# Turning the next expert's rows ahead of the last output product in a mixture-of-experts stage

## The chip, the core and the metric

The kernel runs on one core of a Trainium2 chip. The time is the device time of an execution in microseconds (us), and the figure that counts is the median over several executions. TensorE (PE) multiplies matrices out of SBUF into PSUM; a weight load (PEld) goes ahead of each matmul. VectorE (DVE) and ScalarE (ACT) work elementwise and copy PSUM into SBUF, GpSimd (POOL) issues the indirect transfers here, and SyncE (SP) issues the plain ones.

## What is computed

One layer of a perceiver over 32 sequences of 32 tokens, 512 wide: cross-attention to a context, self-attention, and a feed-forward with 8 experts of which each token takes two. The change touches only the last part:

```python
gate_logits = jnp.einsum('td,ed->te', xf, gate_w)
gate_scores = jax.nn.sigmoid(gate_logits + balance_bias)
topk_scores, topk_idx = jax.lax.top_k(gate_scores, ACTIVE_EXPERTS)
topk_scores = topk_scores / (topk_scores.sum(axis=-1, keepdims=True) + 1e-06)
comb = jnp.zeros((T, NUM_EXPERTS), dtype=x.dtype)
comb = comb.at[jnp.arange(T)[:, None], topk_idx].add(topk_scores)
h = jax.nn.silu(jnp.einsum('td,ehd->teh', xf, w1))
expert_out = jnp.einsum('teh,edh->ted', h, w2)
out = jnp.einsum('te,ted->td', comb, expert_out)
```

There are 1024 tokens, `w1` is 8 x 1024 x 512 and `w2` 8 x 512 x 1024, all in float32. `xf` is the layer's input to this part after a normalization, and the result is added to the residual.

## The kernel before

The kernel computes only the chosen token-expert pairs. While self-attention runs, the normalized row of each token, with its number and its two shares, is scattered by GpSimd into a list per expert in DRAM (`xs_d`). A count near the end of that phase ranks the experts by size, and the place in this ranking, r, has a fixed width, `WIDTH = (384, 352, 288, 288, 288, 224, 192, 160)`; rows beyond these widths go to a branch that is taken only if there are any. The first 256 rows of the largest expert (`EARLY = 2` blocks of 128) are worked on inside the attention phase, between the last tiles of attention: `early_turn`, `early_hidden` eight times, and `early_out`. The names there are `xpe`, `phe` and `poe`.

Then come the experts in order of rank. For each:

- `load_rows` brings its rows into `xs` with the rows on partitions (two buffers).
- `turn_rows` (before: one function) turns each block of up to 128 rows with four TensorE transposes into PSUM (`xpt`), copies them to `xT` (even blocks on ScalarE, odd ones on VectorE, in `evac`, lines 175 to 179), and forms the row numbers `idx` and shares `share` on VectorE.
- `hidden` has eight groups of four matmuls `ph <- xT, w1` (line 1402), a sigmoid on ScalarE (`sg`), and a product on VectorE into `hT`. TensorE needs the whole of `xT` for the first group.
- `output` multiplies `hT` by `w2`. A whole block of 128 rows has eight matmuls of 512 columns (`fpo`, line 1464). A shorter last block is split over the array's columns (`fpq`, line 1369); it comes first, except for the last expert. VectorE scales by the share into `fob` (three buffers), and GpSimd adds the rows to the output with an indirect transfer (`add_rows`, line 195).

The remaining 128 rows of rank 0 (`rest`) have their own way: `hidden_of_block` makes the hidden values with the rows on partitions (`phb`, then `sgb` and `hs`, in two halves), and `turn_hidden` turns them (`hpt`) once the rows of rank 1 have been turned. Its output product stands after the hidden product of rank 1.

Each engine takes its instructions in the order in which the built program lists them. A scheduler forms that order out of the order of the calls; on TensorE it follows the calls in this stage. Buffers rotate: the pool `ps` has four PSUM tiles of one bank each, shared by `phe`, `xpt`, `phb`, `hpt`, `ph` and small ones, and `psf` four for the outputs of `output`. The early outputs before the change take one tile of four banks from `psq`, of which each uses one bank. The weights `w1` and `w2`, 2 MB each, rotate through three buffers; SP's queue issues, for rank r+1, `w1`, the rows and `w2` in this order, each when its buffer is free.

The trace counts two instructions for a float32 matmul call, and one for a transpose: a block's eight `fpo` matmuls show as 16 in it.

Of the kernel before, what the change touches and what calls it, by code (L numbers as in the profile page):

```python
# [9 lines left out]
F32 = mybir.dt.float32  # L10
# [7 lines left out]
P = 128  # L18
# [4 lines left out]
D = 512  # L23
DC = 384
KD = D // P
# [4 lines left out]
NE = 8  # L30
# [5 lines left out]
WIDTH = (384, 352, 288, 288, 288, 224, 192, 160)  # L36
# [16 lines left out]
def tile_perceiver_layer(  # L53
# [28 lines left out]
    ps = ctx.enter_context(tc.tile_pool(name="ps", bufs=4, space=PSUM))  # L82
# [92 lines left out]
    def evac(i, o, src):  # L175
        if i % 2 == 0:
            nc.scalar.copy(o, src)  # L177
        else:
            nc.vector.tensor_copy(o, src)
# [14 lines left out]
    def add_rows(dst, ob, place, n):  # L194
        return nc.gpsimd.indirect_dma_start(  # L195
            out=dst,
            out_offset=bass.IndirectOffsetOnAxis(ap=place, axis=0),
            in_=ob,
            in_offset=None,
            bounds_check=n * ROWS - 1,  # L200
            oob_is_err=True,
            compute_op=ALU.add,
        )

    def load_expert(dst, src, e):

        n = src.shape[1] // 2
        for k in range(2):
            nc.sync.dma_start(
                dst.rearrange("p (h r) -> p h r", h=2)[:, k, :].rearrange(  # L210
                    "p (k f) -> p k f", f=src.shape[2]
                ),
                src[bass.ds(e, 1), ts(k, n), :].rearrange("e (k p) f -> p (e k) f", p=P),
            )

    def expert_w1(e, ewp=ewp):
        w1 = ewp.tile([P, KD * FF], F32, tag="ew", name="w1")
        load_expert(w1, w1T, e)
        return w1.rearrange("p (k f) -> p k f", f=FF)

    def expert_w2(e, ewp=ewp):
        w2 = ewp.tile([P, KF * D], F32, tag="ew", name="w2")
        load_expert(w2, w2T, e)
        return w2.rearrange("p (k f) -> p k f", f=D)

    with ExitStack() as attn:
# [19 lines left out]
        with ExitStack() as xa:  # L246
# [534 lines left out]
            for g in range(NTT + 1):  # L781
                p = g // 2
# [50 lines left out]
        with ExitStack() as sa:  # L833
            wk = sa.enter_context(tc.tile_pool(name="swork", bufs=2))
            psq = sa.enter_context(tc.tile_pool(name="psq", bufs=1, space=PSUM))
# [373 lines left out]

            def early_out():  # L1210
                t = tail["early"]
                pe = psq.tile([P, 4, KD, P], F32, tag="pq", name="poe")
                for c in range(EARLY):
                    po = pe[:, c].rearrange("p k q -> p (k q)")
                    for f in range(KF):
                        nc.tensor.matmul(  # L1216
                            po, t["hT"][f // 4][:, f % 4, ts(c, P)], tail["w2"][0][:, f, :],
                            start=(f == 0), stop=(f == KF - 1),
                        )
                    ob = wk.tile([P, NH * T], F32, tag="aT", bufs=3, name="obe")  # L1220
                    nc.vector.tensor_scalar_mul(ob, po, t["share"][:, c : c + 1])
                    add_rows(out, ob, t["pl"][:, c : c + 1], 1)
# [40 lines left out]
            p = NP - 1  # L1263
# [30 lines left out]
            for f in range(3, KF):  # L1294
                early_hidden(f)
            early_out()


# [5 lines left out]
    hot, eids, w1s, w2s = tail["hot"], tail["e"], tail["w1"], tail["w2"]  # L1304
# [8 lines left out]
    taken = keep.tile(full, I32, name="taken")  # L1313
# [3 lines left out]
    idx = keep.tile(full, I32, name="idx")  # L1317
    nc.gpsimd.iota(
        idx, pattern=[[0, NE], [P, LIST // P]], base=NTT * P, channel_multiplier=1
    )  # L1320
    def parts_of(n):
        return [(c, min(P, n - c * P)) for c in range((n + P - 1) // P)]

    def tails_of(m):

        return [(0, 2 * Q)] * (m // (2 * Q)) + [(m // Q * Q - Q, Q)] * (m // Q % 2)

    def load_rows(e, r0, n):

        xs = fw.tile([P, NB, YW], F32, tag="xs", name="xs")  # L1330
        nb, m = n // P, n % P
        if nb:
            nc.sync.dma_start(
                xs[:, 0:nb, :],
                xs_d[bass.ds(e * LIST + r0, nb * P), :].rearrange("(c p) w -> p c w", p=P),
            )
        if m:
            nc.sync.dma_start(
                xs[0:m, nb, :], xs_d[bass.ds(e * LIST + (r0 + nb * P), m), :]
            )  # L1340
        return xs
# [34 lines left out]

    def turn_rows(r, xs, n, taken, idx):

        share = fw.tile([P, NB], F32, tag="share", name="share")
        xT = fw.tile([P, KD, CAP], F32, tag="xT", name="xT")  # L1380
        for c, m in parts_of(n):
            pt = ps.tile([P, KD, P], F32, tag="ps", name="xpt")
            for k in range(KD):
                nc.tensor.transpose(pt[:, k, 0:m], xs[0:m, c, ts(k, P)], ident[0:m, 0:m])  # L1384
            evac(c, xT[:, :, c * P : c * P + m], pt[:, :, 0:m])
            nc.vector.copy_predicated(
                idx[0:m, c : c + 1], taken[0:m, c : c + 1],
                xs[0:m, c, YI : YI + 1].bitcast(I32),
            )
            sh = fw.tile([P, NE], F32, tag="sh", name="sh")  # L1390
            nc.vector.tensor_mul(sh[0:m], xs[0:m, c, YC : YC + NE], hot[0:m, r, :])
            nc.vector.reduce_sum(share[0:m, c : c + 1], sh[0:m], axis=AX.X)
        return {"n": n, "xT": xT, "share": share, "idx": idx}

    def hidden(t, w1):

# [20 lines left out]
    def hidden_of_block(t, w1):  # L1417

        hs = fw.tile([P, FF], F32, tag="hs", bufs=1, name="hs")
        for h in range(2):  # L1420
            ph = ps.tile([P, D], F32, tag="ps", name="phb")
            for k in range(KD):
                nc.tensor.matmul(  # L1423
                    ph, t["xT"][:, k, 0:P], w1[:, k, ts(h, D)],
                    start=(k == 0), stop=(k == KD - 1),
                )
            sg = fw.tile([P, D], F32, tag="sgb", bufs=1, name="sgb")
            nc.scalar.activation(sg, ph, AF.Sigmoid)
            nc.vector.tensor_mul(hs[:, ts(h, D)], ph, sg)
        t["hs"] = hs  # L1430
# [6 lines left out]
                nc.tensor.transpose(pt[:, k, :], t["hs"][:, ts(h * KD + k, P)], ident)  # L1437
            evac(h, t["hT"][:, h * KD : (h + 1) * KD, 0:P], pt)

    def output(t, w2, short_first=True):  # L1440

        hT, share, idx = t["hT"], t["share"], t["idx"]
        parts = parts_of(t["n"])
        adds = []

        def short():
            for c, m in parts:
                if m < P:
                    for r0, q in tails_of(m):
                        adds.append(  # L1450
                            short_part(
                                hT[:, :, c * P + r0 : c * P + r0 + q],
                                w2, q, *t["spread"].pop(0),
                            )
                        )

        if short_first:
            short()
        for c, m in parts:
            if m < P:  # L1460
                continue
            po = psf.tile([P, D], F32, tag="psf", name="fpo")
            for f in range(KF):
                nc.tensor.matmul(  # L1464
                    po, hT[:, f, ts(c, P)], w2[:, f, :],
                    start=(f == 0), stop=(f == KF - 1),
                )
            ob = fw.tile([P, D], F32, tag="fob", bufs=3, name="fob")
            nc.vector.tensor_scalar_mul(ob, po, share[:, c : c + 1])  # L1469
            adds.append(add_rows(out, ob, idx[:, c : c + 1], 1))  # L1470
        if not short_first:
            short()

            for i, a in enumerate(adds):
                for b in adds[:i]:
                    tc.declare_no_dep(a.ins, b.ins, reason="rows of their own")


    rows_of = {
        0: load_rows(eids[0], EARLY * P, WIDTH[0] - EARLY * P),  # L1480
        1: load_rows(eids[1], 0, WIDTH[1]),
    }
    w2s[1] = expert_w2(eids[1])
    rest = turn_rows(
        0, rows_of.pop(0), WIDTH[0] - EARLY * P, taken[:, 0, EARLY:], idx[:, 0, EARLY:]
    )
    hidden_of_block(rest, w1s.pop(0))
    for r in range(1, NE):
        if r + 1 < NE and r > 1:
            w1s[r + 1] = expert_w1(eids[r + 1])  # L1490
            rows_of[r + 1] = load_rows(eids[r + 1], 0, WIDTH[r + 1])
            w2s[r + 1] = expert_w2(eids[r + 1])
        t = turn_rows(r, rows_of.pop(r), WIDTH[r], taken[:, r], idx[:, r])
        if r == 1:
            turn_hidden(rest)
        hidden(t, w1s.pop(r))
        if r == 1:
            output(rest, w2s.pop(0))
            w1s[2] = expert_w1(eids[2])
            rows_of[2] = load_rows(eids[2], 0, WIDTH[2])  # L1500
            w2s[2] = expert_w2(eids[2])
        output(t, w2s.pop(r), r + 1 < NE)


    over = keep.tile([P, NE + 1], F32, name="over")
# [131 lines left out]
```

## Time and profile before

| what | us |
|---|---|
| median of three runs | 552.19 |
| the runs | 551.84, 552.19, 555.09 |
| the profiled execution | 559.04 |
| its span, first to last instruction | 557.3 |
| TensorE busy in the span | 520.1 |
| VectorE, ScalarE, GpSimd busy | 241.9, 123.2, 106.1 |
| mean granted TensorE clock | 0.985 |

The stages in that execution, by the chain of waits: attention up to about 304 us; the early output products 304.3 to 319.2; the rest of rank 0 and the turning of rank 1, 319.2 to 329.7; then rank 1 to 375.6, rank 2 to 409.4, rank 3 to 443.2, rank 4 to 476.9, rank 5 to 504.0, rank 6 to 527.2, rank 7 to 547.3, and the last row additions to the end. The bounds from 375.6 to 527.2 are the starts of the next expert's `xpt`.

A line of the profile names the program's line (L1402), the engine, the operation, what it writes and reads, how often, and times. A wait is given with the instruction that released it. Matmul ends are modelled, so that consecutive matmuls overlap in the list; the spacing of starts is what a stream of them costs.

### The profile page before, as it was taken

What the parts mean: (1) busy time and instruction counts of PE and PEld (TensorE: products, weight loads), DVE (VectorE), ACT (ScalarE), POOL (GpSimd) and SP (SyncE); (2) the same over time, 40 slices, a digit from 0 to 9 for tenths busy, and PEclk for the clock granted to TensorE, in tenths of its full rate; (3) what the DMA queues carried; (4) which work ended last, traced back from release to release, by engine and by line L of the source; (5) the groups of instructions that cost most, each with busy time, mean ns of one, the idle gap of its engine ahead of it and who ended that gap; (6) DMA issues with size and microseconds to landing.
All of it is one profiled execution on the core that took longest, in us unless ns stands there. A gap on an engine that the chain in (4) does not pass through costs nothing.

```text
span 557.3 us, 11309 instructions
## 1 busy us (share of the span) xinstructions
PE 520.1 (93%) x4718; PEld 337.6 (61%) x4718; DVE 241.9 (43%) x706; ACT 123.2 (22%) x274; POOL 106.1 (19%) x185
## 2 busy tenths in 40 slices
PE   6999998999989999999789899999999999999992
PEld 3655554556675774866368356547567475768571
DVE  6564668655676665778244132203113121223120
ACT  3444434322321412213031021002011020102010
POOL 2323446120001023031202100122111202112102
PEclk9899999999999999999799999999999999999997
DMA  8999977999931002021494250847463455756512
GB/s 279 393 379 403 303 266 269 360 393 386 387 124 39 2 19 100 4 80 41 157 396 160 68 162 9 285 95 231 158 192 114 125 181 158 217 162 198 163 21 28
DMA packets 43648, 104.56 MB, mean 188 GB/s; under 512 B 4002, under 2 KB 7234, under 8 KB 42563
## 3 DMA queue, kind: packets, MB, share of 16 engines
q1 hardware_dynamic: 38994, 94.96, 47.4%
q0 software_dynamic: 4592, 8.78, 7.8%
q8 instruction: 39, 0.64, 0.5%
q14 instruction: 23, 0.18, 0.1%
HBM read 75.55 MB, written 28.18 MB: 186 GB/s over the span
## 4 chain that ended last, share of the span: by engine, by line
PE 68%; DVE 3%; issue 2%; ACT 1%; POOL 0%; POOLq 0%; ACTq 0%
PE ph L1402 18%; PE fpo L1464 15%; PE pp L388 8%; PE ppv L858 4%; PE ppo L934 4%; PE fpq L1369 4%; PE phe L1202 3%; PE poe L1216 3%; PE pos L915 2%; PE pqs L873 1%; PE phb L1423 1%; PE xpt L1384 1%; PE pg L980 1%; ACT xT L177 1%; PE po L671 1%
## 5 line engine op out<-in xcount | busy, mean ns | idle before, releaser
L1402 PE MATMUL ph<-xT,w 128*128 128x288 f32 (+4 forms) x448 | 100.2, 382 | 3.1 <-ACT xT L177 3.1
L1402 PEld LDWEIGHTS ph<-xT,w 128*128 128x128 f32 x448 | 79.0, 190 | 19.6 <-ACT xT L177 3.7
L1464 PE MATMUL fpo<-w,hT 128*128 128x512 f32 x192 | 84.3, 595 | 0.0
L1464 PEld LDWEIGHTS fpo<-w,hT 128*128 128x128 f32 x192 | 35.9, 190 | 43.7 <-issue 43.5
L1408 DVE TENSOR_TENSOR hT<-ph,sg 128x288 f32<-128x288 f32 (+4 forms) x56 | 23.7, 422 | 63.9 <-ACT sg L1407 63.9
L1469 DVE TENSOR_SCALAR fob<-fpo,share 128x512 f32<-128x512 f32 x12 | 9.0, 751 | 75.9 <-PE fpo L1464 75.9
L1407 ACT ACTIVATE sg<-ph 128x288 f32<-128x288 f32 (+4 forms) x56 | 21.5, 384 | 85.0 <-PE ph L1402 83.5
L195 POOL DMA_INDIRECT out_dram<-fob,idx x12 | 18.6, 1548 | 106.3 <-DVE fob L1469 93.5
L934 PE MATMUL ppo<-ao,oT 128*128 128x512 f32 x64 | 31.0, 638 | 2.3 <-DVE oT L922 2.3
L528 DVE BATCH_NORM_STATS2 st<-n 128x6 f32<-128x384 f32 x64 | 32.5, 545 | 0.0
L177 ACT COPY xT<-xpt 128x512 f32<-128x512 f32 (+2 forms) x12 | 6.0, 496 | 112.5 <-PE xpt L1384 112.4
L195 POOL DMA_INDIRECT out_dram<-fob,plc x9 | 13.9, 1546 | 88.9 <-DVE fob L1374 71.2
L483 PE MATMUL pq<-x1T,mq 128*128 128x256 f32 x96 | 24.7, 406 | 0.0
L671 PE MATMUL po<-wvo,uT 128*128 128x512 f32 x48 | 22.4, 602 | 1.2 <-ACT uT L664 1.2
L934 PEld LDWEIGHTS ppo<-ao,oT 128*128 128x128 f32 x64 | 12.9, 205 | 17.4 <-issue 14.5
L1072 POOL DMA_INDIRECT xs_d<-fy,pi x16 | 17.2, 1073 | 30.1 <-DVE pi L1068 20.2
L388 PE MATMUL pp<-syT,ak 128*128 128x256 f32 x96 | 22.4, 385 | 0.3 <-issue 0.3
L1369 PE MATMUL fpq<-w,hT 128*32 128x128 f32 (+1 forms) x576 | 22.3, 309 | 0.0
L388 PE MATMUL pp<-syT,aq 128*128 128x256 f32 x96 | 22.1, 383 | 0.0
L858 PE MATMUL ppv<-av,syT 128*128 128x512 f32 x48 | 21.3, 594 | 0.0
L483 PEld LDWEIGHTS pq<-x1T,mq 128*128 128x128 f32 x96 | 18.5, 202 | 4.1 <-issue 1.2
L1369 PEld LDWEIGHTS fpq<-w,hT 128*32 128x32 f32 x576 | 16.2, 110 | 7.1 <-issue 3.2
(280 smaller groups left out, 734.7 us busy)
## 6 DMA issues: line engine op xcount, KB each, us to landing
xs_d<-zero SPq DMA_DIRECT2D x8, 2112.0 KB, 20.5
w<-in_w1T_dram SPq DMA_DIRECT2D x16, 1024.0 KB, 7.7
w<-in_w2T_dram SPq DMA_DIRECT2D x16, 1024.0 KB, 8.8
nT<-in_ctxT_dram SPq DMA_DIRECT2D x8, 1542.0 KB, 8.2
n<-in_ctx_dram SPq DMA_DIRECT2D x32, 384.0 KB, 5.9
xs<-xs_d SPq DMA_DIRECT2D x4, 528.0 KB, 9.4
x_sb<-in_x_dram SPq DMA_DIRECT2D x8, 256.0 KB, 7.5
out_dram<-x_sb SPq DMA_DIRECT2D x8, 256.0 KB, 2.1
```

Of the source, the lines that this page charges most:

```text
L195: return nc.gpsimd.indirect_dma_start(out=dst, out_offset=bass.IndirectOffsetOnAxis(ap=place, axis=0), in_=ob, in_offset=None, bounds_chec ...
L388: nc.tensor.matmul(pp[:, i, :], w[:, k, ts(e, P)], yT[:, k, :], start=(k == 0), stop=(k == KD - 1),)
L483: nc.tensor.matmul(pq[:, 0 : 2 * P], mq[:, k, ts(c, P)], x1T[:, k, :], start=(k == 0), stop=(k == KD - 1),)
L528: nc.vector.bn_stats(st[:, r, :], n[:, r // 2, r % 2, :])
L671: nc.tensor.matmul(po, uT[:, c, :], wvo[:, c, :], start=(c == 0), stop=(c == KC - 1))
L858: nc.tensor.matmul(pp, st[p]["yT"][:, k, ts(i, P)], av[:, k, :], start=(k == 0), stop=(k == KD - 1),)
L934: nc.tensor.matmul(pp, st[p]["oT", i][:, k].rearrange("p b q -> p (b q)"), ao[:, k, :], start=(k == 0), stop=(k == KD - 1),)
L1369: nc.tensor.matmul(po[ts(g, Q), 0:w], hT[:, f, ts(h, Q)], w2[:, f, ts(j, w)], start=(f == 0), stop=(f == KF - 1),)
L1402: nc.tensor.matmul(ph[:, 0:n], w1[:, k, ts(f, P)], t["xT"][:, k, 0:n], start=(k == 0), stop=(k == KD - 1),)
L1407: nc.scalar.activation(sg[:, 0:n], ph[:, 0:n], AF.Sigmoid)
L1408: nc.vector.tensor_mul(hT[:, f, 0:n], ph[:, 0:n], sg[:, 0:n])
L1464: nc.tensor.matmul(po, hT[:, f, ts(c, P)], w2[:, f, :], start=(f == 0), stop=(f == KF - 1),)
```

## The change

Three things are done. `turn_rows` is divided into `turning`, which takes the tiles, and `turn_parts`, which turns a choice of blocks. `output` takes a function `ahead`, called before the product of its last whole block; for rank r that function turns the rows of rank r+1. The rows of rank 1 have no output before them to go ahead of, and are turned in two pieces: the first block before `hidden_of_block(rest)` and the others after it. And `early_out` takes one tile of `ps` for each of its two products, in place of one tile of four banks for both.

In the built program, ranks 2 to 5 have their transposes between the first and the second `fpo` product of the expert before; ranks 6 and 7, whose predecessors have one whole block, have them between `fpq` and `fpo`. On VectorE the copy into `xT` comes one place earlier, ahead of the last `fob`; the `idx` and `share` operations of a later expert come one `hT` product later; and one copy into `xT` now stands between the two `hs` products. On ScalarE the first copy for rank 1 comes ahead of both `sgb`. The orders on SP and POOL are unchanged.

```diff
             def early_out():
                 t = tail["early"]
-                pe = psq.tile([P, 4, KD, P], F32, tag="pq", name="poe")
                 for c in range(EARLY):
-                    po = pe[:, c].rearrange("p k q -> p (k q)")
+                    po = ps.tile([P, D], F32, tag="ps", name="poe")
                     for f in range(KF):
                         nc.tensor.matmul(
                             po, t["hT"][f // 4][:, f % 4, ts(c, P)], tail["w2"][0][:, f, :],
...
     def turn_rows(r, xs, n, taken, idx):
 
+        t = turning(r, xs, n, taken, idx)
+        turn_parts(t)
+        return t
+
+    def turning(r, xs, n, taken, idx):
         share = fw.tile([P, NB], F32, tag="share", name="share")
         xT = fw.tile([P, KD, CAP], F32, tag="xT", name="xT")
-        for c, m in parts_of(n):
+        return {
+            "n": n, "r": r, "xs": xs, "xT": xT, "share": share, "idx": idx, "taken": taken,
+        }
+
+    def turn_parts(t, which=slice(None)):
+        xs, xT, share = t["xs"], t["xT"], t["share"]
+        r, idx, taken = t["r"], t["idx"], t["taken"]
+        for c, m in parts_of(t["n"])[which]:
             pt = ps.tile([P, KD, P], F32, tag="ps", name="xpt")
             for k in range(KD):
                 nc.tensor.transpose(pt[:, k, 0:m], xs[0:m, c, ts(k, P)], ident[0:m, 0:m])
...
-    def output(t, w2, short_first=True):
+    def output(t, w2, short_first=True, ahead=None):
...
-        for c, m in parts:
-            if m < P:
-                continue
+        blocks = [c for c, m in parts if m == P]
+        for c in blocks:
+            if ahead and c == blocks[-1]:
+                ahead()
             po = psf.tile([P, D], F32, tag="psf", name="fpo")
...
+    t = turning(1, rows_of.pop(1), WIDTH[1], taken[:, 1], idx[:, 1])
+    turn_parts(t, slice(0, 1))
     hidden_of_block(rest, w1s.pop(0))
+    turn_parts(t, slice(1, None))
     for r in range(1, NE):
-        if r + 1 < NE and r > 1:
-            w1s[r + 1] = expert_w1(eids[r + 1])
-            rows_of[r + 1] = load_rows(eids[r + 1], 0, WIDTH[r + 1])
-            w2s[r + 1] = expert_w2(eids[r + 1])
-        t = turn_rows(r, rows_of.pop(r), WIDTH[r], taken[:, r], idx[:, r])
+        n = r + 1
+        if n < NE and r > 1:
+            w1s[n] = expert_w1(eids[n])
+            rows_of[n] = load_rows(eids[n], 0, WIDTH[n])
+            w2s[n] = expert_w2(eids[n])
         if r == 1:
             turn_hidden(rest)
         hidden(t, w1s.pop(r))
         if r == 1:
             output(rest, w2s.pop(0))
-            w1s[2] = expert_w1(eids[2])
-            rows_of[2] = load_rows(eids[2], 0, WIDTH[2])
-            w2s[2] = expert_w2(eids[2])
-        output(t, w2s.pop(r), r + 1 < NE)
+            w1s[n] = expert_w1(eids[n])
+            rows_of[n] = load_rows(eids[n], 0, WIDTH[n])
+            w2s[n] = expert_w2(eids[n])
+        turned = []
+
+        def ahead():
+            if n < NE:
+                turned.append(
+                    turn_rows(n, rows_of.pop(n), WIDTH[n], taken[:, n], idx[:, n])
+                )
+
+        output(t, w2s.pop(r), n < NE, ahead)
+        t = turned[0] if turned else None
```

More of the change, by code (lines that the diff above doesn't have):

```diff
@@ L1392, in turn_rows @@
             nc.vector.reduce_sum(share[0:m, c : c + 1], sh[0:m], axis=AX.X)
-        return {"n": n, "xT": xT, "share": share, "idx": idx}
     def hidden(t, w1):
```

## The prediction, made before the changed kernel ran

> **What bounds the kernel now.** I read the page first: TensorE's row, the slices and the costliest groups. Then the waits of TensorE from 300 us to the end, the chain of waits for the same stretch, and last the timeline of two places.
>
> ```profile
> PE 520.1 (93%) x4718; PEld 337.6 (61%) x4718; DVE 241.9 (43%) x706; ACT 123.2 (22%) x274; POOL 106.1 (19%) x185
> ...
> PE   6999998999989999999789899999999999999992
> ...
> PEclk9899999999999999999799999999999999999997
> ...
> L1402 PE MATMUL ph<-xT,w 128*128 128x288 f32 (+4 forms) x448 | 100.2, 382 | 3.1 <-ACT xT L177 3.1
> ```
>
> TensorE is busy for 93% of the span. Each digit is a slice of 13.9 us; from 320 us on, where the experts are, it never falls below nine tenths until the last slice, and the 8 just before (306 to 320 us) is the end of the early expert. The clock is nine tenths or more there. So in the expert stage only TensorE's own work and its own holes count. The group row shows one kind of hole: 3.1 us before `ph`, ended by ScalarE's copy into `xT`. The waits of TensorE from 300 us on list all of them:
>
> ```profile
> PE ph L1402 <- ACT xT L177: 3.1, 6, 0.7
> PE poe L1216 <- DVE obe L1221: 0.8, 1, 0.8
> PE phb L1423 <- ACT xT L177: 0.7, 1, 0.7
> ```
>
> Columns: waiter, what it waited for, us in all, times, longest. That is 4.6 us in eight waits, the most that a reordering of this stage can give back by this list. In the chain (start us, us, engine, tile, line) they look so:
>
> ```profile
> 304.32 6.88 PE poe L1216 x16
> 311.22 0.76 DVE obe L1221
> 312.03 7.13 PE poe L1216 x16
> ...
> 319.64 0.59 ACT xT L177
> 320.27 7.13 PE phb L1423 x16
> ...
> 375.59 1.25 PE xpt L1384 x12
> 376.86 0.27 ACT xT L177
> 377.13 0.16 issue
> 377.30 4.12 PE ph L1402 x16
> ```
>
> TensorE turns an expert's rows (`xpt`, 1.25 us), has nothing else in its queue, and waits until the copies out of PSUM end. The chain has PE before and after each of these holes, so they lie on the path to the end.
>
> **The change part by part.** All sums are against the profiled execution: 559.04 us, span 557.3 and 1.7 around it. It lies 6.85 us above the median of the three runs shown (552.19). The holes are waits of one instruction for another, tens to hundreds of ns each, and I carry them over to the median unscaled.
>
> *Rows of experts 2 to 7 ahead of the last block's product.* No instruction is added: per expert the same 8 or 12 transposes, copies, `idx` and `share` operations. The built order shows what moves. On TensorE the transposes go ahead of the last 8 `fpo` products (16 matmuls in the trace). On VectorE the copy of the second 128 rows goes ahead of the last `fob`. On ScalarE nothing changes places, and the issues on SP's and POOL's queues are the same in the same order. The holes by expert, from the timeline: 0.47, 0.47, 0.47, 0.70, 0.56, 0.43, sum 3.10. Cover in their new place: one block's product, 7.0 us, against about 1.0 us for the last transpose's landing and its copy. So the holes go whole: -3.10. From the weight-load row the same six waits are 3.7 us, which is the upper end; the lower end is 2.7, if each expert's return from transposes to products costs 0.07 us more than a plain step. That is what the one switch shown costs (eight `hpt` start at 328.57 and `ph` at 329.50, 0.93 instead of 8 times 0.107).
>
> What could be late next? First, the rows themselves, since the transposes come 7 us sooner and the block's product is queued behind them. The `idx` operation on VectorE reads the same rows and shows when they land:
>
> ```profile
> 359.78 0.22 DVE L1386 COPY_PREDICATED_SCALAR idx<-taken,xs 128x1 int32 x1 [2.67 <-DMA xs<-xs_d]
> ```
>
> Expert 2's rows are there at 359.8, and their transposes would start at 368.7 on this clock: 8.9 us to spare. For expert 7 it is 513.3 at the latest against 520.1, 6.8 us; the others lie between or above. Second, VectorE's copy stands behind `fob` of the block before, which waits for the scatter three before it to free its buffer; in this trace every `fob` waited for TensorE (75.9 us of 75.9), and a delay costs only beyond the 5 us or so of cover. Third, the loads of the next weights start at an expert's end as before, but its successor's `ph` now starts 1.7 us sooner relative to that. The `idx` operations of the expert after stand one `hT` product later in VectorE's order, so they wait about as long as before (7.9 us in five waits), and TensorE did not wait for VectorE there. Cost of all three: 0.
>
> *A buffer for each early output.* Two tiles from the general pool of four take the place of the halves of one large tile. The second `poe` product no longer waits for the 0.76 us scaling of the first: -0.84 (312.03 less the end at 311.20). The new tiles take over from `phe` outputs whose readers ended before 302; the two after them in the ring are only written at about 319. No other wait comes in.
>
> *The second expert's rows around the first product of the rest.* Its first four transposes now stand ahead of `phb`. They do not bring `phb` forward: it waits for ScalarE's copy of its own rows, 1.27 us after the first transpose either way, and that copy is still first in ScalarE's queue. The hole of 0.68 us is just filled with 0.43 us of work, which then is missing after `phb`. There it was cover:
>
> ```profile
> 327.25 1.37 PE L1384 MATMUL xpt<-ident,xs 128*128 128x128 f32 x12
> 327.45 0.60 ACT L1428 ACTIVATE sgb<-phb 128x512 f32<-128x512 f32 x1 [2.84 <-PE phb L1423]
> 327.94 1.19 ACT L177 COPY xT<-xpt 128x512 f32<-128x512 f32 x2
> 328.08 0.69 DVE L1429 TENSOR_TENSOR hs<-phb,sgb 128x512 f32<-128x512 f32 x1 [2.74 <-ACT sgb L1428]
> 328.57 1.09 PE L1437 MATMUL hpt<-ident,hs 128*128 128x128 f32 x8
> 329.50 0.79 PE L1402 MATMUL ph<-xT,w 128*128 128x352 f32 x2
> ```
>
> Call E the end of `phb`, 327.25. Now the second half's `hs` runs from E+0.83 to E+1.52, and its four `hpt` come at E+1.75: no wait. In the changed order VectorE has a copy into `xT` (0.69) between the two `hs` products. It can start when four transposes have landed, E+0.63 (as 376.06 follows 375.43 for the same four), ends at E+1.32, and only then comes the second `hs`, to about E+1.92. TensorE, with 8 instead of 12 transposes, is at the second half's `hpt` at E+1.3 and waits to E+1.97; with 0.47 for these four, `ph` starts at E+2.44 instead of E+2.25. So this part costs 0.19. Between -0.43 (no wait) and +0.6 (the copy later still) I take +0.19, worked out from these rows.
>
> Sum: -3.10 - 0.84 + 0.19 = -3.75. Span 553.55, profiled execution 555.3; median 552.19 - 3.75 = 548.4, 0.7% down. From the bounds: -2.7 - 0.84 + 0.6 = -2.9 (549.3), and -3.7 - 0.84 - 0.43 = -5.0 (547.2).
>
> **A rule that speaks against it.** The row: a transpose's mean is 272 ns here, but twelve take 1.25 us in the chain, about 0.105 each, because they overlap. The Trainium skill, "TensorE: Matmul & The Clock Gate", Part 4 (PE-mode transpose), has about 275 ns for one in a kernel, mostly access latency, and says that transposes do not count as busy for the clock gate. By the rule's price, 60 moved transposes that did not overlap among matmuls would add 60 x (0.275 - 0.105) = 10.2, and the sum would be +6.5. By the row it is -3.75. The trace has the step from matmuls into transposes already, at the same spacing and a clock of 1.00 in the windows around every one; only the step back to 512-wide products is not shown. I take the row. For the clock, 1.3 us of transposes between products replace 1.9 us of transposes and hole, so less idleness than now.
>
> **The rivals.**
> 1. *Transposes that don't overlap in their new place* (slower). Place: the six stretches of transposes that now stand among the output products. At 0.272 each: +10.0 - 3.75 = +6.3, about 558.5. It decides from 0.107 + 3.75/60 = 0.17 us each, where the gain is gone; 1% slower needs 0.26. For it: the mean and the rule. Against it: the spacing in the chain. Chance 0.05.
> 2. *The waits come back in another place*: rows, a buffer of `fob`, or a copy that holds up the products after it. It would need 7 us of delay against spare times of 6.8 and more, or a PSUM slot that I missed. The gain is then lost in large part: 551 to 552.5. Chance 0.08.
> 3. *Only the first part is different*: the change of order around `phb` works as its cover says on paper, -0.43 instead of +0.19, and the holes are worth 3.7: 547.2. Chance 0.15. A gain over 5.5 us would need holes that the list of waits doesn't have; 0.07 for that and for a drift of the runs.
> 4. The likeliest, as worked out, 547.6 to 549.6: 0.65.
>
> **How the numbers follow.** About 1% is what a measurement of this kernel can tell from no change; its three runs lie 3.25 us apart. 1% is 5.5 us, so cases 2, 3 and 4 are "within 1%": 0.65 + 0.15 + 0.08 = 0.88, of which I leave 0.01 to slower. Faster 0.07, same 0.87, slower 0.06. The range takes in the bounds 547.2 and 549.3 with the scatter of a median of runs (0.35 us between the lower two of three) and part of case 2: 546.8 to 550.8.
>
> **What would show it.** Right: no wait of `ph` for `xT` in TensorE's list; the second `poe` starts with the first one's end; `fpo` follows `xpt` without a hole, twelve transposes still at 1.25 us; the stage from `poe` to the last `fpq` 3 to 5 us shorter. The small loss would show as a new wait of `hpt` for `hs` of 0.6 to 0.7 us. Wrong: `xpt` waiting for a DMA, `fpo` or `ph` waiting for VectorE, a slice in the expert stage with a lower clock, or transposes spaced by more than 0.17 us.

## The result, and the profile after

| | before | after |
|---|---|---|
| median of 17 runs each (us) | 553.33 | 548.01 |
| lowest to highest | 549.51 to 555.11 | 545.52 to 551.21 |
| profiled execution, span | 559.04, 557.3 | 545.52, 543.8 |

The ratio is 0.9918, with a 95% interval of 0.9896 to 0.9941: 3.3 to 5.8 us less. Forecast were 548.4 us and 0.7% less, with 546.8 to 550.8 as the range. The three runs that the forecast started from have a median 1.1 us below that of all 17, so the 548.0 is closer to 548.4 than the working deserves: from 553.33 the same sum would have given 549.6. A start that was too low and a sum that was too small offset each other, which is luck. The sum to judge is -3.75 us, and where each part of it came from. One execution among all the runs below, 552.71 of the kernel with all rows of rank 1 first, was in a slower state and is left out of that kernel's median and ratio.

First the page of the changed kernel: engine totals, slices, the granted clock by slice, and the group of `ph`.

```profile
PE 514.4 (95%) x4718; PEld 335.1 (62%) x4718; DVE 241.7 (44%) x706; ACT 123.3 (23%) x274; POOL 106.2 (20%) x185
...
PE   5999998989999999999889999999999999999992
...
PEclk9999999999999999999999999999999999999998
...
L1412 PE MATMUL ph<-xT,w 128*128 128x288 f32 (+4 forms) x448 | 99.7, 381 | 0.0
```

The idle time before `ph` is 0.0 where it was 3.1. But the two spans differ by 13.5 us, three times what the waits could give. The clock row shows one difference outside the experts: the 7 of the kernel before in the slice at 265 us is a 9 here. So the two executions have to be compared by stage. I measure the *expert stage* from the start of the first `poe` product to the start of the last group of `fpq`:

| us | before | after | difference |
|---|---|---|---|
| first instruction to first `poe` | 304.16 | 295.53 | -8.63 |
| first `poe` to first `xpt` | 14.84 | 13.73 | -1.11 |
| first `xpt` to first `ph` | 10.50 | 10.79 | +0.29 |
| first `ph` to the rest's `fpo` | 19.79 | 19.75 | -0.04 |
| the rest's `fpo` to the last `fpq` | 195.33 | 191.72 | -3.61 |
| the expert stage | 240.46 | 235.99 | -4.47 |
| last `fpq` to the end | 12.7 | 12.3 | -0.4 |

TensorE's waits from 290 us on, after (waiter, what it waited for, us, times, longest):

```profile
PE hpt L1447 <- DVE hs L1439: 0.7, 1, 0.7
PE phb L1433 <- ACT xT L177: 0.2, 1, 0.2
```

These two lines are the whole list. The wait of `hpt` for `hs` is new, and it is the small loss that the prediction had worked out. The chain of waits shows it, and a turning ahead of the last block (start us, us, engine, tile, line):

```profile
295.69 13.73 PE poe L1215 x32
309.43 0.45 PE xpt L1395 x4
309.90 0.59 ACT xT L177
310.54 7.13 PE phb L1433 x16
317.67 0.45 PE xpt L1395 x4
318.15 0.69 DVE xT L179
318.84 0.61 DVE hs L1439
319.45 0.14 issue
319.58 0.63 PE hpt L1447 x4
320.21 4.74 PE ph L1412 x16
...
352.17 7.06 PE fpo L1476 x16
359.23 1.23 PE xpt L1395 x12
360.47 7.06 PE fpo L1476 x16
367.53 3.88 PE ph L1412 x16
```

The 32 matmuls of `poe` are now one item, with no `obe` between. The chain leaves TensorE after the four transposes that follow `phb`, goes over VectorE's copy of them into `xT` and the second `hs`, and comes back at `hpt`. For expert 2, `fpo`, `xpt`, `fpo` and `ph` follow each other with nothing between, and the twelve transposes still take 1.23 us.

### The profile page after: what moved, and what is told of

Read it like the earlier page. It is cut to its first block, busy times and chain, and to the rows that moved or that the text cites. A ratio compares the mean times of both kernels' runs of the same rounds, so it can differ in the third digit from the quotient of the medians.

```text
span 543.8 us, 11311 instructions
## 1 busy us (share of the span) xinstructions
PE 514.4 (95%) x4718; PEld 335.1 (62%) x4718; DVE 241.7 (44%) x706; ACT 123.3 (23%) x274; POOL 106.2 (20%) x185
## 4 chain that ended last, share of the span: by engine, by line
PE 54%; DMA 8%; issue 6%; DVE 4%; POOL 1%; ACT 1%; POOLq 0%; ACTq 0%; DVEq 0%
PE ph L1412 12%; PE fpo L1476 10%; PE pp L388 8%; DMA out_dram<-fob,idx 5%; PE ppo L934 4%; PE ppv L858 4%; PE phe L1202 3%; DMA out_dram<-fob,plc 3%; PE poe L1215 3%; PE fpq L1368 2%; PE pqs L873 1%; PE pos L915 1%; PE phb L1433 1%; PE pg L980 1%; PE xpt L1395 1%
## 5 line engine op out<-in xcount | busy, mean ns | idle before, releaser
L934 PE MATMUL ppo<-ao,oT 128*128 128x512 f32 x64 | 28.5, 595 | 2.4 <-DVE oT L922 2.4
L483 PE MATMUL pq<-x1T,mq 128*128 128x256 f32 x96 | 23.0, 384 | 0.0
L483 PEld LDWEIGHTS pq<-x1T,mq 128*128 128x128 f32 x96 | 17.4, 190 | 3.6 <-issue 1.2
```

The costliest lines, as they stand in the source:

```text
L483: nc.tensor.matmul(pq[:, 0 : 2 * P], mq[:, k, ts(c, P)], x1T[:, k, :], start=(k == 0), stop=(k == KD - 1),)
L934: nc.tensor.matmul(pp, st[p]["oT", i][:, k].rearrange("p b q -> p (b q)"), ao[:, k, :], start=(k == 0), stop=(k == KD - 1),)
```

## The experiments

Nine more kernels were run, and the changed one again. The time of a single execution is of little use, since the part up to `poe` varies by 9 us from one to another; the expert stage of the trace is what is compared. It was 235.99 us again in a second profile of the changed kernel. The diffs show the lines that matter, with `...` for lines left out.

| kernel | expert stage, us | against before | against after |
|---|---|---|---|
| early buffers alone | 239.35 | -1.11 | |
| rows ahead alone | 236.86 | -3.60 | |
| divided turning alone | 240.71 | +0.25 | |
| all but the divided turning | 235.75 | -4.71 | -0.24 |
| the changed kernel again | 235.99 | -4.47 | 0.00 |
| all rows of rank 1 first | 234.62 | -5.84 | -1.37 |
| cover of one step | 236.12 | -4.34 | +0.13 |
| rows in pieces | 236.02 | -4.44 | +0.03 |
| each transpose twice | 241.49 | +1.03 | +5.50 |
| rows loaded last | 242.38 | +1.92 | +6.39 |

### One part at a time

The kernel before, with the early buffers alone:

```diff
-                pe = psq.tile([P, 4, KD, P], F32, tag="pq", name="poe")
                 for c in range(EARLY):
-                    po = pe[:, c].rearrange("p k q -> p (k q)")
+                    po = ps.tile([P, D], F32, tag="ps", name="poe")
```

> The kernel before with one part of the change: a tile of the common pool for each early output. Measured by the expert stage, from the start of the first poe product to the start of the last group of fpq: 240.46 us before, 235.99 with all of the change. Theory (three separate holes, their gains add up): poe waits no more for obe, the stage is 0.84 (the wait as listed) to 1.11 us (as the change's trace has it, from starts) shorter, 239.35 to 239.6; the wait of phb and the six of ph stay at 0.7 and 3.1. Rival (the gain comes from a common cause, such as the clock or the times of the transfers, and not from this wait): the stage moves by less than 0.4 or by more than 2 us.

Measured: 239.35, and in its list of waits only that of `poe` is gone:

```profile
PE ph L1401 <- ACT xT L177: 3.1, 6, 0.7
PE phb L1422 <- ACT xT L177: 0.7, 1, 0.7
```

The rows ahead alone (the change, with the early outputs and rank 1 put back):

```diff
...
-    turn_parts(t, slice(0, 1))
     hidden_of_block(rest, w1s.pop(0))
-    turn_parts(t, slice(1, None))
+    turn_parts(t)
```

> Only the rows of experts 2 to 7 are turned ahead of the last block's product; the early outputs and the rows of rank 1 are as before. Theory: the six waits of ph for xT go and nothing else changes, the stage goes from 240.46 to about 236.9 (3.54 from starts), or 237.4 if only the listed 3.10 is won; hpt has no wait. Rival (common cause): a gain of less than 2.5 or more than 4.5 us.

Measured: 236.86, 3.60 less; the waits of `ph` are gone, those of `poe` (0.8) and `phb` (0.7) are there, and none is new.

The divided turning alone (the early outputs as before, and the turning after the output):

```diff
...
-        output(t, w2s.pop(r), n < NE, ahead)
+        output(t, w2s.pop(r), n < NE)
+        ahead()
```

> Only the turning of rank 1 is divided around phb; all else as before. Theory: this part costs. phb is not sooner, the four transposes are missed as cover after it, VectorE's copy stands between the two hs products, and hpt waits 0.7 us for hs: the stage is 0.2 to 0.3 us longer, 240.66 to 240.76, and from the first xpt to the first ph it takes 10.79 instead of 10.50. Rival (the division gains, and the new wait is a consequence of the other parts): the stage is 0.2 to 0.45 shorter, no wait of hpt for hs.

Measured: 240.71, 0.25 more than before; first `xpt` to first `ph` 10.78. Its waits:

```profile
PE ph L1413 <- ACT xT L177: 3.1, 6, 0.7
PE poe L1216 <- DVE obe L1221: 0.8, 1, 0.8
PE hpt L1448 <- DVE hs L1440: 0.7, 1, 0.7
PE phb L1434 <- ACT xT L177: 0.2, 1, 0.2
```

The wait of `phb` falls by 0.5 and one of 0.7 comes in. So the loss belongs to this part alone. The three differences, -1.11 - 3.60 + 0.25, sum to -4.46, and the whole change has -4.47: the gains add up, as three separate holes would.

### Is the earlier start of `poe` part of the change?

> The changed kernel again, as a measure for the two below. Theory: the expert stage, from the start of the first poe product to the start of the last fpq group, is 235.99 us within 0.2, whatever the clock does in the attention stages; the median is 0.7 to 0.9% under the kernel before. Rival (part of the 13.5 us between the two profiled spans belongs to the change, in the attention stages): the span up to the first poe is again some 8 us shorter than in the kernel before.

Measured: the median is 547.42 against 553.46, ratio 0.9906 (0.9877 to 0.9935); the stage is 235.99. But the first `poe` came at 296.88, some 7 us sooner than in the kernel before, which is what the rival expected. Other kernels decide it, which have the whole change in front of `poe`. The cover of one step, the rows in pieces and the rows loaded last (all below) reach `poe` at 303.74, 302.99 and 304.62, as late as the kernel before; each transpose twice reaches it at 298.43. The windows from 260 to 280 us, of the kernel before, the change, and the cover of one step, in this order (busy us of PE, PEld, DVE, ACT, POOL, then the granted clock, DMA share, GB/s):

```profile
260.00:280.00 20.00, 15.58 (x350) 8.81 (x337) 9.78 (x44) 1.42 (x3) 4.38 (x6) 0.83 0.38 137
```

```profile
260.00:280.00 20.00, 17.07 (x308) 10.21 (x307) 12.29 (x46) 3.08 (x5) 5.08 (x6) 1.00 0.70 251
```

```profile
260.00:280.00 20.00, 15.51 (x294) 8.55 (x284) 9.66 (x40) 1.21 (x2) 4.39 (x6) 0.83 0.40 147
```

The lower clock comes with the change as well as without it. It accounts for some 3.4 us by an estimate (0.17 of the 20 us). A second difference is a wait of `pos`, an attention product, for which the trace shows no releaser. It stands in TensorE's list up to 295 us of the kernel before (first line) and of the cover of one step (second), and not at all in the two profiles of the change:

```profile
PE pos L915 <- issue: 3.6, 8, 0.5
PE pos L915 <- issue: 3.3, 7, 0.5
```

Of all twelve profiles, the seven with this wait, with the change or without it, reach `poe` at 301.8 us or later, and the five without it at 298.6 or sooner. Together with a clock of 0.94 in the first 30 us, where the change had 1.00 (1.8 us by the same estimate), this is about all of the 8.63. These differences come with the execution or its chip, not with the change, so I don't count the 8.63 us to it. Whole times agree: beside the kernel before on the same chip, single executions of the cover of one step and of the rows in pieces took 3.1 and 4.8 us less (554.29 against 557.43, 554.28 against 559.06), not 13. And the medians of 17 runs, less the 1.7 around the span and the part from `poe` to the end in the profile, leave 298.4 us up to `poe` before and 298.0 after (548.01 - 1.72 - 248.27), as far as that part of one trace stands for all runs. The six executions on two of the chips all came to `poe` late and the four on a third all early. What brings on the wait and the lower clock stays open.

### The middle part taken out, and replaced

> The change without its middle part: the rows of rank 1 are turned in one piece after phb, as before. Theory: the stage is 0.2 to 0.3 us shorter than with the change, about 235.7; the wait of phb is back at 0.7, that of hpt is gone. In the median that is less than can be told. Rival (the division gains): the stage is 0.2 to 0.45 us longer.

This kernel is the change with the diff of the second experiment. Measured: 235.75, 0.24 less than with the change, the wait of `phb` back at 0.7 and that of `hpt` gone. The time, 548.49 (0.9925, 0.9898 to 0.9951), can't tell it from the change.

The version that was to have neither hole:

```diff
...
-    turn_parts(t, slice(0, 1))
-    hidden_of_block(rest, w1s.pop(0))
-    turn_parts(t, slice(1, None))
+    turn_parts(t)
+    hidden_of_block(rest, w1s.pop(0))
...
-        if r == 1:
-            turn_hidden(rest)
-        hidden(t, w1s.pop(r))
+        hidden(t, w1s.pop(r), (lambda: turn_hidden(rest)) if r == 1 else None)
...
+            if f == 3 and between:
+                between()
```

> A version meant to have neither hole: all rows of rank 1 are turned before phb, and the turning of the rest's hidden values (hpt) goes between the fourth and the fifth group of ph. Theory: neither phb nor hpt nor ph waits, the stage is about 1.2 us shorter than with the change, 234.8 (phb starts 1.7 us after the first xpt, ph follows phb directly, and 0.87 us of hpt come later). Rival (the copies of hT take the place of hT products on VectorE and ScalarE, and ph waits for a PSUM tile): waits of ph in place of that of hpt, the stage at 235.5 or more.

Measured: 234.62, 1.37 less than with the change, and TensorE has no wait at all from 300 us on. Its timeline on TensorE (start us, us, operation, count):

```profile
310.60 1.80 PE L1395 MATMUL xpt<-ident,xs 128*128 128x128 f32 x16
312.24 7.06 PE L1435 MATMUL phb<-w,xT 128*128 128x512 f32 x16
319.13 4.90 PE L1412 MATMUL ph<-xT,w 128*128 128x352 f32 x16
...
329.42 1.04 PE L1449 MATMUL hpt<-ident,hs 128*128 128x128 f32 x8
330.29 9.63 PE L1412 MATMUL ph<-xT,w 128*128 128x352 f32 x32
```

Sixteen transposes now fill the time of the copy that `phb` waits for, and `hpt` comes 10 us after `phb`, when its `hs` has long been there. The time, 547.29 (0.9890, 0.9854 to 0.9926), is below that of the kernel before and not to be told from that of the change beside it, 547.42. In the stage it is the better version.

### What the move needs, and what it costs

Cover of one step: the rows are turned before the last of the eight steps of the block's product.

```diff
-            if ahead and c == blocks[-1]:
-                ahead()
             po = psf.tile([P, D], F32, tag="psf", name="fpo")
             for f in range(KF):
+                if ahead and c == blocks[-1] and f == KF - 1:
+                    ahead()
```

> All of the change, but the rows ahead are turned before the last of the eight steps of the last block's product, not before the first: cover 0.86 us instead of 6.9. Theory (a hole is only the landing of the last transposes and one copy, 0.43 to 0.7 us): the cover is still enough, the stage stays within 0.4 us of 235.99 and ph has no wait of more than 0.1 for xT. Rival (the copies need more, since the scaling of the block before and the small operations stand ahead of them on VectorE): waits of ph for xT of 0.3 to 0.6 us each come back, the stage is 2 to 3.5 us longer.

Measured: 236.12, no wait of `ph`. TensorE at expert 2 (start us, us, operation, count):

```profile
373.28 1.40 PE L1395 MATMUL xpt<-ident,xs 128*128 128x128 f32 x12
374.61 1.12 PE L1476 MATMUL fpo<-w,hT 128*128 128x512 f32 x2
375.57 0.65 PE L1412 MATMUL ph<-xT,w 128*128 128x288 f32 x2
```

A cover of one step, 0.96 us here, costs 0.13 in all; of the 7 us that the change gives, most is to spare.

Rows in pieces (the blocks before steps 0, 2 and 4 of the product):

```diff
+                if ahead and c == blocks[-1] and f in (0, 2, 4):
+                    ahead(f // 2)
...
```

> All of the change, but the blocks of rows are turned one at a time before steps 0, 2 and 4 of the last block's product: 15 stretches of transposes among the products instead of 6. It prices the step from transposes back to products and the other way. Theory (a step costs at most some 0.1 us): the stage is 0 to 0.9 us longer than 235.99. Rival (TensorE must run empty at each change of kind, some 0.17 us for the way in and the way out each): 9 more stretches cost 3 us, the stage 239.

Measured: 236.02. Nine more stretches cost 0.03 us in all, so the step from the transposes of a whole block to products and back is free here, to what can be read. The last, shorter block of each expert was followed by a product already, so this run does not price that step.

Each transpose of experts 2 to 7 twice:

```diff
-            for k in range(KD):
+            for k in [*range(KD)] * (2 if t["n"] < CAP and r > 1 else 1):
```

> All of the change, and each transpose of the rows of experts 2 to 7 is issued twice, the second writing the same values: 60 more. It prices a transpose where the change has put it. Theory (they overlap there as elsewhere): 0.095 to 0.11 us each, the stage 5.7 to 6.6 us longer, 241.7 to 242.6. Rival of the prediction (each at its full length among the products): 0.272 each, 16.3 us longer, 252.3.

Measured: 241.49, so 5.50 us for 60 transposes, 0.092 each; a little under the theory's range, since 24 of them have fewer than 128 rows. From start to start those with 128 rows take 0.109 us, those with 96 take 0.082, and those with 64 or 32 take 0.062: 36, 4 and 20 of them make 5.5. The rival of the prediction, 0.272 each, falls. The timeline of expert 2 has 24 of them in 2.44 us, from start to start:

```profile
361.97 2.52 PE L1395 MATMUL xpt<-ident,xs 128*128 128x128 f32 x24
364.41 7.13 PE L1476 MATMUL fpo<-w,hT 128*128 128x512 f32 x16
```

Rows loaded last:

```diff
-            rows_of[n] = load_rows(eids[n], 0, WIDTH[n])
             w2s[n] = expert_w2(eids[n])
+            rows_of[n] = load_rows(eids[n], 0, WIDTH[n])
```

> All of the change, but for each rank the rows are loaded after w2 instead of before it, so that they are issued only at the end of the hidden product of the expert before. It takes away the 7 to 9 us to spare that the prediction read off. Theory (the rows' landing is the limit of how far ahead they can be turned): xpt waits for its rows, by some 3 us for ranks 3 to 5 and 6 to 8 us for ranks 6 and 7, the stage 15 to 25 us longer, and the kernel slower than before. Rival (the rows land soon enough in any order): no wait of xpt, the stage within 1 us of 235.99.

Measured: 242.38, 6.39 more than with the change and 1.92 more than before. The mechanism is there:

```profile
PE xpt L1395 <- DMA xs<-xs_d: 3.5, 4, 1.5
PE xpt L1395 <- SPq L1582: 1.4, 1, 1.4
```

The size was overrated: 15 to 25 was expected. For 528 KB the median from issue to landing was 7.5 us. And the scheduler moved the transposes of some experts by one or more steps into the block's product (for ranks 3 and 4 to after its first step, for ranks 6 and 7 to after the fourth and the sixth), so a wait of less than the whole delay was left. The two lines hold 4.9 of the 6.4 us. From starts it is nearly all: the six steps from a product to the transposes behind it are 0.68, 1.76, 0.96, 2.09, 1.04 and 2.01 us, where 0.43 is the step without a wait, so 6.0 are lost there.

## Why the prediction was right, point by point

*The holes before `ph`.* Right in place and mechanism, and mis-sized: -3.10 in the sum, -3.60 alone on the chip, near the upper bound of 3.7. The term took the idle time of TensorE as the list gives it, which starts at a modelled end. From starts, the two traces give three parts for experts 2 to 7 together. From the first transpose to the next product it is 10.18 us before and 6.67 after, so -3.51: the listed end of an expert's last transpose is 0.22 to 0.25 us after its start, while with the change the next product starts 0.08 to 0.15 after it. The first two groups of `ph`, behind a hole before and behind a product after, take 20.45 and 20.00, so -0.45. And the `fpo` products take 83.21 and 83.56, so +0.35: that is the return from transposes to products, which the lower bound had put at 0.07 each. The three make -3.61.

*The early outputs.* -0.84 in the sum, -1.11 measured, for the same reason and one more, visible in the weight loads of the kernel before after its hole:

```profile
312.03 0.30 PEld L1216 LDWEIGHTS poe<-w,hTe 128*128 128x128 f32 x2 [1.67 <-DVE obe L1221]
312.56 0.19 PEld L1216 LDWEIGHTS poe<-w,hTe 128*128 128x128 f32 x1 [0.24 <-issue]
312.99 0.19 PEld L1216 LDWEIGHTS poe<-w,hTe 128*128 128x128 f32 x1 [0.24 <-issue]
```

The first row holds two loads, 0.11 us apart: the second matmul's load, which in the stream is done one matmul ahead, starts here behind the first. The matmuls themselves start at 312.03, 312.56 and 312.99. Starts are 0.43 us apart in the stream, but 0.53 after the hole: a restart costs 0.1 more. With 0.17 for the modelled end (a `poe` matmul is listed with 0.60 us, where the starts are 0.43 apart), 0.84 becomes 1.11.

*The rows around `phb`.* Right, and the sign was the point: +0.19 in the sum, +0.25 alone. Step by step from E, the end of `phb`, where the next transposes start (317.51): the copy was to start at E+0.63 and did at E+0.64; `hs` was to end at E+1.92 and did at E+1.93; `hpt` at E+1.97, did at E+2.07; `ph` at E+2.44, did at E+2.54. The return from `hs` to `hpt` had been put 0.1 too short.

*What could be late.* Nothing was: no wait of `xpt`, `fpo` or `ph`. The rows of expert 7 landed at 502.7 for transposes at 507.4, so 4.7 us to spare. The prediction had 6.8 from times of the old order, and rows loaded last show that the rows can become the limit. The operations `idx` wait 9.7 us for rows on VectorE, where it was 7.9 and the forecast had about as long; TensorE did not wait for VectorE there, as forecast.

*The rule on transposes.* The row was the better guide: 0.092 us each where the change puts them, and no lower clock in any expert slice. The about 275 ns that the Trainium skill has in "TensorE: Matmul & The Clock Gate", Part 4, for a bf16 transpose of 128x128 agree as a length with the 272 that the float32 ones of whole blocks have here (258 over all widths); as a price in a stream they would have given a slower kernel.

*The sum.* -3.75 against -4.47 in the stage and -5.3 in the medians (interval -5.8 to -3.3). The rest of the medians is within their interval, and I know no mechanism of the change for it. Of the rivals, the first falls with the price of a transpose, the second with the empty list of waits of `ph`, `fpo` and `xpt`, and the third with the +0.25 of the divided turning.

## What to carry to other kernels

An in-order engine that waits for a copy of what it has just made wants independent work placed between the two, as little as one step of a product here, 0.96 us at expert 2. The same move can cost where it takes away cover: ask of each instruction that is moved what it was hiding in its old place, before counting what it fills in its new one. And price a hole from start to start, against the spacing of the undisturbed stream, not from the listed idle time.

## What the runs showed that was not expected

The parts of the expert stage that two kernels share repeat to 0.01 us: first `poe` to first `xpt` is 13.73 or 13.74 in all eight kernels with the new early buffers, and 191.72 from the rest's `fpo` to the last `fpq` in four kernels and a repeat. In the same executions the time up to `poe` ran from 295.5 to 304.6 us, with a granted clock of 0.70 to 1.00 in the window from 260 to 280 us; from 290 to 340 us it was 1.00 in every one. So a stage taken from a single trace settled differences of 0.1 us that the medians of 17 runs could not.
